# Softmax sums of an attention block taken off TensorE: transfers through DRAM and 32x32 transpositions in place of ones-matmuls

## The chip, the cores and the metric

The kernel runs on one core of a Trainium2 chip. The metric is the time of one execution on the device in microseconds (us). The profile is one execution as the hardware profiler records it. Its engines are PE (TensorE matmuls), PEld (TensorE weight loads, which overlap PE), DVE (VectorE), ACT (ScalarE), POOL (GpSimd) and SP (SyncE, which starts most of the transfers).

## The reference

The input x is 8 images of 64 channels and 64x64 pixels, float32. Layer 0 is attention over the 4096 pixels of each image, with a second, "unary" softmax that doesn't depend on the query:

```python
q = q - q_mean                      # q, k, v = 1x1 convolutions of x
k = k - k_mean
sim = softmax(einsum('bcn,bcm->bnm', q, k) / 8, axis=2)
out = einsum('bnm,bcm->bcn', sim, v)
unary = softmax(einsum('bc,bcm->bm', q_mean, k))
out = out + einsum('bcm,bm->bc', v, unary)[:, :, None]
x = x + out
```

Layer 1 takes the sign of the result, convolves it with binary weights of sizes 1, 3 and 5 with batch norm, adds the three, multiplies by a gate that is computed from the mean over each whole image, and adds its own input.

## The kernel before

Two images form a pair: image 0 has its channels on partitions 0 to 63, image 1 on 64 to 127. There are 4 pairs. For each pair there are 8 query blocks (`qb`) of 512 queries, so 32 blocks, numbered `g`. Within a block a loop of 32 slots `j` runs over the keys, 128 at a time. In each slot:

- `scores` computes the logits of 128 keys with 512 queries of both images into a PSUM tile `ps` (two buffers), four 64x64 matmuls in float32 (line 466), and ACT turns them into `e` with an exp (line 477). The pool `ep` has four buffers of `e`.
- `weighted` multiplies the values `v` with the `e` of the slot before and accumulates in `acc` (line 485), one buffer of two PSUM banks.
- `summed` adds that `e` to `es` on DVE (lines 498 and 500). At the end of the block `es` holds, for each query, 128 partial sums over keys, one on each partition.

Scores of slot j are issued before `weighted` and `summed` of slot j-1, so PE does not wait for the exp of its own slot. All orders are written out by hand: `attend` makes for each block a plan `at` of extra work by slot (`put(slot, function, ...)`), and each engine takes its instructions in that order.

At slot 0 of block g stands the work on older blocks. `weighted_out` copies `acc` of block g-1 to SBUF on ACT (line 507). `both` calls `mix_rows`: the query projection of block g+1 and, from g=3 on, the convolutions of block g-3, some 100 short bf16 matmuls (line 680). Their results lie in `z` tiles: two that share the `ps` pool, `z3` that takes the two banks of `acc`, and `z_5d` and `z1` in the two-buffer pool `ps_m`. ACT starts the row tile `sb` from `z_5d` (line 695) and copies `z3` out to `es_z` (`hold_rows`, line 720). DVE adds the others (`add_rows`, line 713); the parts kept in `es_z` are added later (`add_held`), and `end_rows` adds `z1` (line 729).

Then follow the sums of block g-1. `sums` multiplies `es` with ones on TensorE (line 516): four matmuls with 32 output columns each, one for each half of the queries of each image, so that each sum stands on 32 partitions. `reciprocals` inverts 128x256 values from PSUM on DVE in two halves (line 529, slots 4 and 6). `spread` copies them with eight SBUF to SBUF transfers on SP to the tile `r`, in which all 64 channels of an image have the reciprocals of its 512 queries (slot 7). `check_block` takes two signs with accumulation on ACT (line 409), which decide at the end whether a safe path is needed. `added` and `finish` (slots 10 and 12, lines 559 to 564) make x + out in `x2`. `signs_wide` and `signs` make the convolution's input from it, and `row_sums` its differences of rows (slots 17 and 19).

In blocks qb=2 the next pair's x is loaded. In blocks qb=3 `mean_part` sums it on DVE (line 278, slots 14, 18, 22, 26), and the eight output tiles of the pair before are finished on DVE and stored (`store`, line 796, every third slot from 3 on). At qb=4 `mean_scores` uses the sums. In blocks qb=4 to 7 `values` makes the next pair's value tiles, and `unary_part` adds the weighted values into `vu`. At qb=0 of that pair, `unary_end` sums `vu` over partitions, with four 128x1 matmuls, one for each 128 columns (line 355).

Of the kernel before, what the change touches and what calls it, by code (L numbers as in the profile page):

```python
# [18 lines left out]
F32 = mybir.dt.float32  # L19
# [3 lines left out]
ALU = mybir.AluOpType  # L23
AX = mybir.AxisListType
PSUM = bass.MemoryType.PSUM

P = 128
C = 64
# [3 lines left out]
QB = 512  # L32
NQ = N // QB
# [11 lines left out]
def conv_seq_kernel(ctx, tc, x, wq, wk, wv, vecs, w1, w3, w5, wtap, gw, out):  # L45
    nc = tc.nc
    n_pairs = x.shape[0] * x.shape[1] // P
    xf = x.rearrange("b c h w -> (b c) (h w)")
    of = out.rearrange("b c h w -> (b c) (h w)")
    img = [slice(0, C), slice(C, P)]  # L50
# [4 lines left out]
    ep = ctx.enter_context(tc.tile_pool(name="ep", bufs=4))  # L55
    fp = ctx.enter_context(tc.tile_pool(name="fp", bufs=1))
    sm = ctx.enter_context(tc.tile_pool(name="small", bufs=2))
    ps_s = ctx.enter_context(tc.tile_pool(name="ps_s", bufs=2, space=PSUM))
    ps_a = ctx.enter_context(tc.tile_pool(name="ps_a", bufs=1, space=PSUM))
    ps_m = ctx.enter_context(tc.tile_pool(name="ps_m", bufs=2, space=PSUM))  # L60

    def m_tile(name):
        return ps_m.tile([P, QB], F32, tag="m", name=name)
# [44 lines left out]
    make_identity(nc, ident)  # L108
    wu = cp.tile([P, P], F32, tag="wu", name="wu")
    nc.gpsimd.memset(wu, 0.0)  # L110

    fit = cp.tile([P, 2, n_pairs * (NQ + 1)], F32, tag="fit", name="fit")
    lim = cp.tile([P, 3], F32, tag="lim", name="lim")
# [140 lines left out]
    class Pair:  # L254
# [88 lines left out]
                nc.vector.tensor_tensor(self.vu, old, t, ALU.add)  # L343

        def unary_sum(self):
            su = self.tile(sm, "su2", 0, (P, 2))
            nc.vector.tensor_reduce(su, self.eu, AX.X, ALU.add)
            self.eub = self.tile(sm, "cl", "s")[:, 0:P]
            for b in range(2):
                nc.vector.tensor_scalar(self.eub[:, img[b]], ones[:, 0:C], su[:, b : b + 1], None, ALU.mult)  # L350

        def unary_end(self):
            po = self.po = m_tile(f"po_{self.name}")
            for t in range(4):
                nc.tensor.matmul(  # L355
                    po[:, 0:1], self.vu[:, bass.ts(t, P)], ones[:, 0:1], start=(t == 0), stop=(t == 3)
                )
            nc.tensor.matmul(po[:, 1:2], self.eub, ones[:, 0:1], start=True, stop=True)

        def unary_out(self):  # L360
# [145 lines left out]
            for c in parts:  # L506
                nc.scalar.copy(self.acc[qb][:, :, c], acc[:, :, c])  # L507

        def sums(self, qb):

            self.sums_p = m_tile(f"su_{self.name}_{qb}")
            es = self.es.pop(qb)
            for b in range(2):
                for h in range(2):
                    i = 2 * b + h
                    nc.tensor.matmul(  # L516
                        self.sums_p[32 * i : 32 * i + 32, 0 : QB // 2],
                        ones[:, 0:32],
                        es[:, b, bass.ts(h, QB // 2)],
                        start=True,  # L520
                        stop=True,
                        tile_position=(0, 32 * i),
                    )

        def reciprocals(self, qb, part):
            if part == 0:
                self.rc = self.tile(fp, "rc", qb, (P, QB // 2))
            c = bass.ts(part, P)
            nc.vector.reciprocal(self.rc[:, c], self.sums_p[:, c])  # L529

        def spread(self, qb):
            self.r[qb] = self.tile(fp, "r", qb)
            for b in range(2):
                for s in range(2):
                    for h in range(2):
                        i, o = C * b + 32 * h, C * b + 32 * s
                        nc.sync.dma_start(
                            out=self.r[qb][o : o + 32, bass.ts(h, QB // 2)], in_=self.rc[i : i + 32, :]
                        )


        def sums_wide(self, qb):
# [23 lines left out]
            )  # L566

        def check_block(self, qb, side):
            self.check(self.rc, int(self.name) * NQ + qb, (side,))


        def join(self):
# [358 lines left out]
    def attend(pairs):  # L931
# [9 lines left out]
        def plan(g):  # L941


            at = {}

            def put(i, f, *a):
                at.setdefault(i, []).append((f, a))

            pr, qb = divmod(g, NQ)

            def nx():
                return pairs[pr + 1]

            if g >= 1:
                p, b = block(g - 1)
                put(0, p.weighted_out, b)
            if qb == 3 and pr >= 1:
                put(0, pairs[pr - 1].gate)
            if qb == 4 and pr + 1 < n_pairs:
                put(0, lambda: nx().mean_scores())  # L960
                put(0, lambda: nx().mean_scores_out())
                put(1, lambda: nx().value_weights())
            if qb == 0 and pr >= 1 or g == 1:
                put(0, pairs[g // NQ].unary_end)
                put(0, pairs[g // NQ].unary_out)
            if g == 2:
                put(0, mean_rows_out)
            def both():
                q = block(g + 1) if g + 1 < n_blocks else None
                if g == 0:  # L970
                    mix(q, None)
                else:
                    mix_rows(q, rows(g - 3) if g >= 3 else None)

            put(0, both)
            if g >= 3:
                p3, b3 = block(g - 3)
                put(2, p3.add_held, b3, "AB")
                put(3, p3.add_held, b3, "SD")
                put(4, p3.end_rows, b3)  # L980
            if g >= 1:
                put(0, p.sums, b)
                for part in range(2):
                    put(4 + 2 * part, p.reciprocals, b, part)
                put(7, p.spread, b)
                put(8, p.check_block, b, 0)
                put(10, p.check_block, b, 1)
                put(10, p.added, b)
                put(12, p.finish, b)
                put(15, p.signs_wide, b, 2)  # L990
                put(17, p.signs_wide, b, 1)
                put(19, p.signs, b)
            if g + 2 < n_blocks:
                put(2, lambda: block(g + 2)[0].copy_x(block(g + 2)[1], (g + 2) // NQ * P))
            if 2 <= g < n_blocks - 1:
                p2, b2 = block(g - 2)
                put(17, p2.row_sums, b2)
                put(19, p2.row_sums3, b2)
            if g == n_blocks - 4:
                put(14, p.copy_tile)  # L1000
            if qb == 2 and pr >= 1:
                put(20, pairs[pr - 1].gate_mean)
            if qb == 3 and pr >= 1:
                for i in range(NQ):
                    put(3 + 3 * i, pairs[pr - 1].store, i, rows_of(pr - 1))
            if g == 0:
                for i in range(NQ):
                    put(max(4 * i - 1, 0), pairs[0].values, i)
                    put(4 * i + 1, pairs[0].unary_part, i)
                put(31, pairs[0].unary_sum)  # L1010
                for i, n in enumerate((2, 1, 0)):
                    put(8 + 8 * i, weight_mean, n)
                    put(12 + 8 * i, weight_scale, n)
            if g == 1:
                put(10, norms)
                put(11, mean_rows)
            if g == 2:
                for n in range(3):
                    put(12 + 5 * n, centre, n)
                    put(14 + 5 * n, weight_signs, n)  # L1020
                for i in range(2):
                    put(26 + 2 * i, weight_combinations, KS[1 + i])
            if pr + 1 < n_pairs:
                if qb == 2:
                    def begin():
                        pairs[pr + 1] = Pair(str(pr + 1), load_x(str(pr + 1), rows_of(pr + 1)))

                    put(1, begin)
                if qb == 3:
                    for c in range(4):  # L1030
                        put(14 + 4 * c, lambda c=c: nx().mean_part(c, quarters[c]))
                if qb >= 4:
                    for h in range(2):
                        i = 2 * (qb - 4) + h
                        put(14 + 8 * h, lambda i=i: nx().values(i))
                        put(17 + 8 * h, lambda i=i: nx().unary_part(i))
                    if qb == NQ - 1:
                        put(28, lambda: nx().unary_sum())
            if g == n_blocks - 1:
                put(1, pairs[-1].join)  # L1040
                put(22, lambda: mix(None, rows(n_blocks - 3), one_bank, score_banks))
                put(27, lambda: mix(None, (pairs[-1], pairs[-1].joint_rows(0, 6, 0)), one_bank, score_banks))
            return at
# [79 lines left out]

    nb_ = sm.tile([P, 1], F32, tag="nb", name="nb")
    nc.vector.tensor_reduce(nb_, fit, AX.XY, ALU.add)
    nc.vector.tensor_scalar(nb_, nb_, n_pairs * (NQ * QB + 2.0) + QB, None, ALU.is_equal)
    pb = m_tile("pb")
    nc.tensor.matmul(pb[:, 0:1], ones, nb_, start=True, stop=True)
    good = sm.tile([P, 1], I32, tag="good", name="good")
# [121 lines left out]
```

## Time and profile before

| | before |
|---|---|
| median of 3 runs | 1973.69 us (1970.32 to 1974.4) |
| run with the profile | 1970.24 us, span 1968.1 us |
| granted TensorE clock | 0.997 |
| SP transfers `r<-rc` (spread) | 248 of 32 KB, 1.9 us to landing |
| SP transfers `xc<-in_x` | 60 of 64 KB, 2.4 us to landing |
| SP transfers `out<-sb` | 28 of 256 KB, 2.1 us to landing |

In a line of a group the columns are: line of the kernel, engine, operation, written tile <- read tiles, shapes (partitions x elements), number of instructions, then busy time in us with the mean duration of one in ns, then the idle time of the engine just before them with what ended it. A wait is put down to what came last by the profile.

### The profile page before, as it was taken

The page shows a single profiled execution, that of the slowest core. Times are in us where ns is not written, and L with a number is a line of the kernel's source. Part 1 is how long each engine was busy: PE and PEld are TensorE (multiplying, and loading weights), DVE is VectorE, ACT ScalarE, POOL GpSimd, SP SyncE. Part 2 cuts the span into 40 slices and gives each one's busy share as a digit, 9 for nine tenths or more (in the row PEclk, how much of TensorE's full clock was granted, in tenths as well). Part 3 has the DMA queues.
Part 4 walks back from the last instruction along what each step waited for, and adds up shares of the span by engine and source line. Part 5 has one row for each costly group of instructions (what it writes and reads, how often), then busy time and mean ns, then how long its engine had stood idle before and what let it go on. Part 6 is the DMA issues. An engine that isn't in the chain of part 4 may idle for free.

```text
span 1968.1 us, 48733 instructions
## 1 busy us (share of the span) xinstructions
PE 1945.9 (99%) x21120; PEld 766.8 (39%) x21120; DVE 1627.1 (83%) x1976; ACT 1262.8 (64%) x1474; POOL 5.9 (0%) x26
## 2 busy tenths in 40 slices
PE   9999999999999999999999999999999999999997
PEld 4333343343333333343433333343343333333334
DVE  7878988888887798888788878888888888878876
ACT  5667666666666666666666665666666666666663
POOL 0000000000000000000000000000000000000000
PEclk9999999999999999999999999999999999999998
DMA  3010000000001010000002001000000000100001
GB/s 99 10 48 18 16 19 10 18 13 16 18 15 56 18 55 16 18 10 16 16 15 61 14 29 40 16 18 14 14 13 18 16 18 31 40 17 20 20 12 45
DMA packets 43373, 47.96 MB, mean 24 GB/s; under 512 B 16000, under 2 KB 32912, under 8 KB 43024
## 3 DMA queue, kind: packets, MB, share of 16 engines
q1 hardware_dynamic: 42400, 43.59, 8.4%
q8 instruction: 167, 2.74, 0.6%
q10 hardware_dynamic: 720, 1.18, 0.2%
q14 instruction: 54, 0.44, 0.1%
q0 software_dynamic: 32, 0.01, 0.0%
HBM read 14.89 MB, written 8.39 MB: 12 GB/s over the span
## 4 chain that ended last, share of the span: by engine, by line
PE 92%; DVE 5%; issue 1%; ACT 1%; DMA 0%; DVEq 0%; SPq 0%; ACTq 0%
PE ps L466 42%; PE acc L485 42%; PE z L680 4%; DVE es L500 4%; PE su L516 1%; PE pq L451 1%; PE pv L308 1%; PE z L751 1%; ACT e L477 1%; PE z_5d L680 0%; DMA x<-in_x 0%; DVE sb L796 0%; DVE sb L713 0%; PE warm L152 0%; PE po L355 0%
## 5 line engine op out<-in xcount | busy, mean ns | idle before, releaser
L477 ACT ACTIVATE e<-ps 128x1024 f32<-128x1024 f32 x1024 | 1049.8, 1025 | 619.1 <-PE ps L466 590.9
L500 DVE TENSOR_TENSOR es<-es,e 128x1024 f32<-128x1024 f32 x960 | 1171.2, 1220 | 184.4 <-ACT e L477 146.8
L466 PE MATMUL ps<-q,x 64*64 64x512 f32 x8192 | 1067.7, 591 | 0.9 <-DVE kb L162 0.9
L485 PE MATMUL acc<-e,v 64*64 64x512 f32 x8192 | 1064.2, 589 | 0.7 <-ACT e L477 0.3
L485 PEld LDWEIGHTS acc<-e,v 64*64 64x64 f32 x8192 | 309.5, 131 | 572.1 <-ACT e L477 307.0
L466 PEld LDWEIGHTS ps<-q,x 64*64 64x64 f32 x8192 | 307.8, 133 | 543.7 <-issue 287.9
L713 DVE SCALAR_TENSOR_TENSOR sb<-z,frac,sb 128x256 f32<-128x256 f32 x87 | 39.2, 478 | 62.6 <-PE z L680 62.6
L680 PE MATMUL z<-e,wt 64*64 64x256 bf16 x754 | 85.3, 272 | 0.1
L680 PE MATMUL z<-ec,wt 64*64 64x256 bf16 x754 | 85.3, 272 | 0.0
L680 PEld LDWEIGHTS <-wt 64*64 64x64 bf16 x1508 | 77.3, 106 | 1.1 <-issue 0.3
L680 PEld LDWEIGHTS <-wc 64*64 64x64 bf16 x1218 | 67.7, 107 | 3.6 <-issue 0.6
L498 DVE TENSOR_TENSOR es<-e,e 128x1024 f32<-128x1024 f32 x32 | 39.2, 1225 | 33.3 <-ACT e L477 33.3
L713 DVE SCALAR_TENSOR_TENSOR sb<-es_z,frac,sb 128x256 f32<-128x256 f32 x145 | 62.2, 480 | 0.0
L680 PE MATMUL z<-ec,wc 64*64 64x256 bf16 x464 | 62.0, 274 | 0.0
L529 DVE RECIPROCAL rc<-su 128x128 f32<-128x128 f32 x62 | 59.1, 953 | 0.0
L695 ACT ACTIVATE sb<-z_5d,shift,frac 128x256 f32<-128x256 f32 x58 | 29.6, 561 | 45.9 <-PE z_5d L680 45.9
L596 ACT ACTIVATE s<-x,vec 128x512 bf16<-128x512 f32 (+2 forms) x66 | 46.1, 702 | 5.2 <-DVE x L564 5.2
L680 PE MATMUL z<-e,wc 64*64 64x256 bf16 x319 | 45.4, 273 | 0.0
L458 DVE TENSOR_SCALAR q<-pq,mx 128x256 f32<-128x256 f32 x60 | 27.0, 480 | 16.7 <-PE pq L451 16.2
L507 ACT COPY o<-acc 128x1024 f32<-128x1024 f32 (+2 forms) x33 | 32.3, 981 | 1.2 <-PE acc L485 1.2
L409 ACT ACTIVATE ck<-rc,lim 128x256 bf16<-128x256 f32 x62 | 30.9, 498 | 0.0
L720 ACT COPY es_z<-z 128x1024 f32<-128x1024 f32 x29 | 29.3, 1012 | 0.0
(150 smaller groups left out, 698.3 us busy)
## 6 DMA issues: line engine op xcount, KB each, us to landing
r<-rc SPq DMA_DIRECT2D x248, 32.0 KB, 1.9
x<-in_x SPq DMA_DIRECT2D x15, 512.0 KB, 5.8
out<-sb SPq DMA_DIRECT2D x28, 256.0 KB, 2.1
ec<-e SPq DMA_DIRECT2D x29, 153.0 KB, 2.4
xc<-in_x SPq DMA_DIRECT2D x60, 64.0 KB, 2.4
ec<-e SPq DMA_DIRECT2D x29, 132.0 KB, 2.3
y<-y SPq DMA_DIRECT2D x30, 64.0 KB, 1.9
w_tap<-in_wtap SPq DMA_DIRECT2D x2, 560.0 KB, 9.8
```

The source lines that it names most:

```text
L409: nc.scalar.activation(junk[:, 0:w], r, AF.Sign, bias=lim[:, side : side + 1], scale=1.0 - 2.0 * side, accum_out=fit[:, side, i : i + 1],)
L466: nc.tensor.matmul(ps[img[h], b, :], self.x[img[b], bass.ds(j * P + h * H, H)], self.q[qb][img[b], :], start=True, stop=neg is None,)
L477: nc.scalar.activation(e, ps, AF.Exp, scale=1.0 / 8.0)
L485: nc.tensor.matmul(self.acc[qb][img[b], h, :], self.v[img[h], j, img[b]], e[img[h], b, :], start=(j == 0), stop=(j == NK - 1),)
L498: nc.vector.tensor_tensor(self.es[qb], self.first, e, ALU.add)
L500: nc.vector.tensor_tensor(self.es[qb], self.es[qb], e, ALU.add)
L507: nc.scalar.copy(self.acc[qb][:, :, c], acc[:, :, c])
L529: nc.vector.reciprocal(self.rc[:, c], self.sums_p[:, c])
L596: nc.scalar.activation(sy[n][0][:, rows, pad : pad + HH], self.x2[qb][:, r0 * HH : r1 * HH].rearrange("p (h w) -> p h w", w=HH), AF.Sign, ...
L680: nc.tensor.matmul(z[img[b], :].rearrange("p (h w) -> p h w", w=HH), taps[img[h], c * C : c * C + C], src[:, first : first + 3 * step + 1 ...
L695: nc.scalar.activation(sv[:, :, t, :], z.rearrange("p (j w) -> p j w", w=HH), AF.Identity, bias=shift, scale=frac[5][:, t : t + 1],)
L713: nc.vector.scalar_tensor_tensor(out, z.rearrange("p (j w) -> p j w", w=HH), by, out, ALU.mult, ALU.add)
```

## The change

The sums over keys leave TensorE. `es` has 128 partitions of partial sums for 1024 queries (2 images x 512). `send` writes it to DRAM, and `gather` reads it back in four transfers of 128 KB, so that each of the four groups of 32 partitions holds one quarter of the queries (256), with four values per query in each partition. `fold` adds the four on DVE, transposes squares of 32x32, adds the 32 elements of each row, which leaves 8 sums on each partition, takes the reciprocal of these, and transposes them back spread over 32 columns. `spread` writes one row of each group to DRAM and reads it back onto all 64 partitions of an image, with three transfers in place of eight.

The tile that receives the gathered sums comes from the pool of the `e` tiles. The check works on 8 values per partition. `add_held` and `end_rows` move to later slots, the `mean_part` calls move from qb=3 to qb=2 for pairs other than the first, and `vu` is folded to 128 columns on DVE, so that one matmul takes the place of four.

```diff
         def unary_sum(self):
+            for w in (2 * P, P):
+                nc.vector.tensor_tensor(
+                    self.vu[:, 0:w], self.vu[:, 0:w], self.vu[:, w : 2 * w], ALU.add
+                )
...
-            for t in range(4):
-                nc.tensor.matmul(
-                    po[:, 0:1], self.vu[:, bass.ts(t, P)], ones[:, 0:1], start=(t == 0), stop=(t == 3)
-                )
+            nc.tensor.matmul(po[:, 0:1], self.vu[:, 0:P], ones[:, 0:1], start=True, stop=True)
...
-        def sums(self, qb):
...
-        def reciprocals(self, qb, part):
...
+        def send(self, qb):
+            self.sent = self.tile(dp, "es", qb, (4, 32, 4, QB // 2))
+            nc.sync.dma_start(
+                out=self.sent.rearrange("g i q c -> (g i) (q c)"),
+                in_=self.es.pop(qb).rearrange("p b c -> p (b c)"),
+            )
+
+        def gather(self, qb):
+            self.parts = self.tile(ep, "e", f"parts_{qb}", (P, 4, QB // 2))
+            for q in range(4):
+                nc.sync.dma_start(
+                    out=self.parts[32 * q : 32 * q + 32, :, :],
+                    in_=self.sent[:, :, q, :].rearrange("g i c -> i g c"),
+                )
+
+        def fold(self, qb):
+            f, t = self.tile(fp, "fold", qb, (P, QB // 2)), self.parts[:, 0, :]
+            nc.vector.tensor_reduce(f, self.parts.rearrange("p g c -> p c g"), AX.X, ALU.add)
+            nc.vector.transpose(out=t, in_=f)
+            nc.vector.tensor_reduce(
+                rec, t.rearrange("p (k i) -> p k i", i=32), AX.X, ALU.add
+            )
+            nc.vector.reciprocal(rec, rec)
+
+            self.rc = self.tile(fp, "rc", qb, (P, QB // 2))
+            nc.vector.transpose(out=self.rc, in_=rec.unsqueeze(2).broadcast_to([P, 8, 32]))
 
         def spread(self, qb):
+            rows = self.tile(dp, "rc", qb, (4, QB // 2))
+            nc.sync.dma_start(out=rows, in_=self.rc[0:P:32, :])
             self.r[qb] = self.tile(fp, "r", qb)
             for b in range(2):
-                for s in range(2):
-                    for h in range(2):
...
+                nc.sync.dma_start(
+                    out=self.r[qb][img[b], :],
+                    in_=rows[2 * b : 2 * b + 2, :].rearrange("s c -> (s c)").unsqueeze(0).broadcast_to([C, QB]),
+                )
...
         def check_block(self, qb, side):
-            self.check(self.rc, int(self.name) * NQ + qb, (side,))
+            self.check(rec, int(self.name) * NQ + qb, (side,))
...
                 put(0, p.weighted_out, b)
+                put(0, p.send, b)
+                put(0, p.gather, b)
...
-                put(2, p3.add_held, b3, "AB")
-                put(3, p3.add_held, b3, "SD")
-                put(4, p3.end_rows, b3)
+                put(4, p3.add_held, b3, "AB")
+                put(6, p3.add_held, b3, "SD")
+                put(8, p3.end_rows, b3)
             if g >= 1:
-                put(0, p.sums, b)
-                for part in range(2):
-                    put(4 + 2 * part, p.reciprocals, b, part)
-                put(7, p.spread, b)
+                put(3, p.fold, b)
+                put(5, p.spread, b)
                 put(8, p.check_block, b, 0)
...
-                if qb == 3:
+                if qb == (3 if pr == 0 else 2):
                     for c in range(4):
                         put(14 + 4 * c, lambda c=c: nx().mean_part(c, quarters[c]))
```

More of the change, by code (lines that the diff above doesn't have):

```diff
@@ L57, in conv_seq_kernel @@
     sm = ctx.enter_context(tc.tile_pool(name="small", bufs=2))
+    dp = ctx.enter_context(tc.tile_pool(name="dram", bufs=2, space=bass.MemoryType.DRAM))
     ps_s = ctx.enter_context(tc.tile_pool(name="ps_s", bufs=2, space=PSUM))
@@ L110, in conv_seq_kernel @@
     nc.gpsimd.memset(wu, 0.0)
+    rec = cp.tile([P, 8], F32, tag="rec", name="rec")
     fit = cp.tile([P, 2, n_pairs * (NQ + 1)], F32, tag="fit", name="fit")
@@ L507, in weighted_out @@
                 nc.scalar.copy(self.acc[qb][:, :, c], acc[:, :, c])
-        def sums(self, qb):
-            self.sums_p = m_tile(f"su_{self.name}_{qb}")
-            es = self.es.pop(qb)
-            for b in range(2):
-                for h in range(2):
[L515 to L523, printed above, removed]
@@ L525, in reciprocals @@
-        def reciprocals(self, qb, part):
[L526 to L529, printed above, removed]
+        def send(self, qb):
[4 more added lines that the diff above has]
+            )
@@ L531, in spread @@
         def spread(self, qb):
+            rows = self.tile(dp, "rc", qb, (4, QB // 2))
+            nc.sync.dma_start(out=rows, in_=self.rc[0:P:32, :])
             self.r[qb] = self.tile(fp, "r", qb)
             for b in range(2):
-                for s in range(2):
[L535 to L539, printed above, removed]
+                nc.sync.dma_start(
+                    out=self.r[qb][img[b], :],
+                    in_=rows[2 * b : 2 * b + 2, :].rearrange("s c -> (s c)").unsqueeze(0).broadcast_to([C, QB]),
+                )
@@ L1125, in conv_seq_kernel @@
     nc.vector.tensor_reduce(nb_, fit, AX.XY, ALU.add)
-    nc.vector.tensor_scalar(nb_, nb_, n_pairs * (NQ * QB + 2.0) + QB, None, ALU.is_equal)
+    nc.vector.tensor_scalar(nb_, nb_, n_pairs * (16.0 * NQ + 2.0) - 16.0 + 2 * QB, None, ALU.is_equal)
     pb = m_tile("pb")
```

## The prediction

> **What bounds the kernel now.** I read the page's busy shares first, then the chain that ended last, then the groups of instructions, and last the timeline of one start of a block, since the change acts there.
>
> ```profile
> PE 1945.9 (99%) x21120; PEld 766.8 (39%) x21120; DVE 1627.1 (83%) x1976; ACT 1262.8 (64%) x1474; POOL 5.9 (0%) x26
> ...
> PE 92%; DVE 5%; issue 1%; ACT 1%; DMA 0%; DVEq 0%; SPq 0%; ACTq 0%
> ```
>
> TensorE holds 92% of the chain, so matmul time that is removed can count in full, and VectorE at 83% has room on average. The 5% on DVE is not spread evenly: in the list of the chain's pieces it lies in two stretches, 677 to 732 us and 1161 to 1216 us. These are the blocks qb=3 of pairs 1 and 2. From the starts of the conv products I read 58.96 us for a plain block, 60.0 with value tiles, 61.9 with the unary term, but 63.2 and 63.6 for those two. The groups that the change touches:
>
> ```profile
> L516 PE MATMUL su<-es,ones 128*32 128x256 f32 x248 | 19.8, 391 | 0.5
> L529 DVE RECIPROCAL rc<-su 128x128 f32<-128x128 f32 x62 | 59.1, 953 | 0.0
> L355 PE MATMUL po<-ones,vu 128*128 128x1 f32 x32 | 4.2, 253 | 0.0
> L278 DVE TENSOR_REDUCE xs<-x 128x1 f32<-128x1024 f32 x14 | 17.0, 1214 | 2.0 <-DMA x<-in_x 2.0
> ```
>
> And a block's start, from the timeline (start, duration, engine, line, operation, tiles, count, idle before):
>
> ```profile
> 792.83 1.23 DVE L500 TENSOR_TENSOR es<-es,e 128x1024 f32<-128x1024 f32 x1 [0.49 <-ACT e L477]
> ...
> 796.43 1.02 ACT L695 ACTIVATE sb<-z_5d,shift,frac 128x256 f32<-128x256 f32 x2 [1.02 <-PE z_5d L680]
> ...
> 797.23 0.27 PE L680 MATMUL z<-e,wt 64*64 64x256 bf16 x1
> 797.40 1.01 ACT L720 COPY es_z<-z 128x1024 f32<-128x1024 f32 x1
> ...
> 797.51 0.64 PE L516 MATMUL su<-es,ones 128*32 128x256 f32 x8
> 797.61 0.88 DVE L713 SCALAR_TENSOR_TENSOR sb<-z,frac,sb 128x256 f32<-128x256 f32 x2 [1.96 <-PE z L680]
> ...
> 798.08 1.09 PE L466 MATMUL ps<-q,x 64*64 64x512 f32 x8
> ...
> 798.99 1.04 PE L485 MATMUL acc<-e,v 64*64 64x512 f32 x8
> ```
>
> The reader is to see: the sums stand between the last conv product and the next scores on PE; the next `weighted` (798.99) writes the `acc` banks, which hold the conv's z3 until ACT's copy L720 ends at 797.40 + 1.01 = 798.41.
>
> [...] The trace, whose transfers start on SP, has 1.9 us for 32 KB, 2.1 for a 256 KB store and 4.3 for the first of four queued 512 KB loads[...]. [...] The built order has that wait: the gather on SP waits for the landing of send. So the two latencies add. [...] No transpose is in this trace.
>
> **The change, part by part.**
>
> *Sums off TensorE.* Without them the first scores follow the last products: groups of products start 0.11 us apart, so 797.23 + 0.11, with some fill 797.4, instead of 798.08: 0.7 us. But `weighted` would then be due at 797.4 + 0.91 = 798.3, and the banks come free at 798.41, plus 0.06 for the signal (e ends 791.07, weights start 791.13) and about 0.1 for weights: 798.58. Before it began at 798.99. I take 0.40 us a block, not 0.7: the sums stood half in the shade of the z3 copy. The following scores (about 799.44) need the banks whose last reader is L713, ended 799.26: no wait. 26 blocks (29 with convs less the three with stores) by 0.40 = 10.4 us. The first two blocks have no conv: 2 x 0.6 = 1.2 us.
>
> *Fold on VectorE.* Reduction of 1024 elements 1.22, [...] reciprocal of 8 some 0.18 (a 128x1 one takes 0.17)[...]; each waits for the one before, 0.06 as between the dependent adds: 2.9 us. It replaces two reciprocals spaced 0.87: 1.74. So +1.15 us a block. Bounds: 2.3 if all but the reduction run at 0.3; 4.6 if the strided reduction and the transpositions take twice per element. [...] An ordinary block has DVE near 50 us busy in 59 to 60, and by its middle DVE has caught up again (824.84 waits for ACT), so this is hidden behind PE. Queued behind the fold are the adds of e tiles, for which the exps wait through the four e buffers: an exp four tiles later needs the add. An exp starts every 1.72 us, and exp plus add take 2.3, so the slack is 4 x 1.72 - 2.3 = 4.6 us plus PE's own slack of about 0.4. By adding up the DVE rows from 799.3 on, the lag at slot 12 is about 3 us: held.
>
> *Transfers.* es is complete at 792.83 + 1.23 = 794.06. Send moves 512 KB: [...] by the 256 KB store 2.1 + 0.8 = 2.9; upper end 4.3. Then four gather issues at about 0.63 (as the eight r issues, 5.0 us) put the fourth 1.9 us after; it lands in about 2.4 (as xc), upper end 3.5 in 1 KB pieces. Sum 0.1 + 3.0 + 1.9 + 2.4 = 7.4 us: 801.5; upper end 9.9: 803.9. The fold stands in DVE's order behind the add of e tile 2, which ends near 802.7, so it finds its data. What waits: `parts` is an e buffer, and in the built order it passes to e tile 5, whose exp waits for the fold's second reduction. Fold 802.7 + 2.2 = 804.9; that exp is due about 805.7 (806.16 before, less 0.4). 0.8 us to spare, 1.2 with PE's slack; so the fold may begin as late as 803.9. Spread is two more latencies, 2 + 3 us from 805.6, and r is used seven slots later, near 819: hidden. The check on 8 columns saves ACT 0.6 us, off the path.
>
> *Mean sums from qb=3 to qb=2.* In the stretch from 677.08 to 733.3 DVE worked without a pause, 56.2 us. Out go four reductions spaced 1.13 (702.10 to 703.23): 4.5; in comes 1.15: 52.9, starting near 676.6, so to 729.5. PE's own pace would have the last add end at 671.51 + 58.96 - 0.61 - 0.40 = 729.46. So these blocks become about even, 59.4 on average of 63.4: 2 x 4.0 = 8.0 us. The third store block, pair 3, has no mean sums and took 58.96; I charge it 0.3. Block qb=2 gets 4.5 and has no stores (eight spaced 0.67, 5.3): 52.1, below 52.9, hidden.
>
> *Unary term.* Three of four 128x1 matmuls go: 1459.25 to 1460.14 for four, so 0.66 a pair, 2.6 us over four. Two small adds are hidden at slot 28 of DVE.
>
> Sum: 10.4 + 1.2 + 8.0 - 0.3 + 2.6 = 21.9 us. 1973.69 - 21.9 = 1952 us.
>
> **The rivals.** A: the transfers come late. Fifth exp, and with it PE, wait in all 31 blocks. If the gather lands at 805.5, 1.6 us after the limit, 31 x 1.6 = 50 us: 1952 + 50 = 2002, slower than before. For it: two chained latencies on 512 KB, pieces of 1 KB, DVE blocked meanwhile. Against: my upper end is 803.9. B: the fold is at its dear end, 4.6 us. Ordinary blocks lose about 0.5 by the release of the buffer (26 x 0.5 = 13), store and mean blocks 1 us more each (5): 1970. C: the z3 copy doesn't bind and PE gains 0.9 a block, the 0.64 of the sums and the 0.29 that the view gives as the wait of their weights for ACT L695: 26 x 0.5 = 13 more: 1939. Against it: L720 can start no earlier than L695 ends.
>
> **How the numbers follow.** Forecast 0.62, A 0.14, B 0.14, C 0.10. The range goes from 1938, with C, to 1971, with B; it leaves out A and the tails, some 0.18. Faster by over 0.2% means below 1969.7: the forecast, C and over half of B, 0.82. Same 0.05, from B and a slight A. Slower 0.13, from A.
>
> **What would show it.** Right: no L516 group; PE still above 98%; `weighted` after z3 waiting for ACT L720 with a real gap; the fold's reduction without idle time for a DMA; blocks at 58.6 and 59.6; the qb=3 blocks near 59.4. Wrong: idle DVE before the fold released by a DMA, an ACT wait for DVE at e tile 5 in every block, or plain blocks at 58.96 or more; or a fold of over 4 us.

## The result and the profile after

The changed kernel takes 1956.14 us (median of 4 runs, 1955.96 to 1956.36) against 1974.05 us of the kernel before (1970.32 to 1975.08), measured beside it. The ratio is 0.9913, 95% interval 0.9896 to 0.993: 17.9 us faster, where 21.9 were forecast. The spans of the two profiles differ by less, 1968.1 to 1953.9 = 14.2 us. The profile of before is that of its shortest run (1970.24 us), and its runs spread over 5 us, those of the changed kernel over 0.4. The sums below, block by block, are of these two traces, so they must come to 14.2.

From the page of the changed kernel, engines, chain and two groups:

```profile
PE 1927.4 (99%) x20848; PEld 810.3 (41%) x20848; DVE 1683.2 (86%) x2077; ACT 1249.1 (64%) x1474; POOL 5.9 (0%) x26
...
PE 87%; DVE 6%; ACT 5%; issue 1%; DMA 1%; SPq 0%; DVEq 0%; ACTq 0%
...
L533 DVE TENSOR_REDUCE fold<-e_parts 128x256 f32<-128x1024 f32 x31 | 60.7, 1958 | 3.6 <-DMA e_parts<-es 3.6
L732 ACT COPY es_z<-z 128x1024 f32<-128x1024 f32 x29 | 29.3, 1011 | 0.0
```

PE is still busy all the time, but it holds 87% of the chain and no longer 92%: ACT came in with 5%, of which the start of `sb` and the copy of z3 make 2.9. The fold's first reduction takes 1.96 us, far from the 1.22 assumed; waiting for transfers costs VectorE only 3.6 us before 3 of 31 folds (g=1, 2 and 4). Where time is waited for, from the view of waits of the changed kernel (who <- for whom: total us, times, longest):

```profile
PEld acc L489 <- ACT es_z L732: 28.3, 29, 1.0
ACT e L481 <- DVE es L504: 16.9, 20, 1.3
ACT e L481 <- DVE rec L535: 8.1, 6, 2.6
PEld pm L288 <- DVE xm L286: 5.3, 3, 2.3
DVE fold L533 <- DMA e_parts<-es: 3.6, 3, 1.8
```

Every one of the 29 blocks with convolutions waits with the weights of its first `weighted` for the z3 copy. The exps wait for DVE in a few blocks, and the fold's end (L535) in six. Now the start of a plain block (timeline of the changed kernel, columns as before):

```profile
793.86 1.01 ACT L732 COPY es_z<-z 128x1024 f32<-128x1024 f32 x1
...
794.92 0.21 PEld L489 LDWEIGHTS acc<-e,v 64*64 64x64 f32 x8 [1.00 <-ACT es_z L732]
794.92 1.09 PE L489 MATMUL acc<-e,v 64*64 64x512 f32 x8
795.24 0.48 DVE L725 SCALAR_TENSOR_TENSOR sb<-z,frac,sb 128x256 f32<-128x256 f32 x1
795.84 0.24 PEld L470 LDWEIGHTS ps<-q,x 64*64 64x64 f32 x8 [0.71 <-issue]
795.87 1.09 PE L470 MATMUL ps<-q,x 64*64 64x512 f32 x8
...
799.21 1.96 DVE L533 TENSOR_REDUCE fold<-e_parts 128x256 f32<-128x1024 f32 x1
801.21 0.45 DVE L534 STREAM_TRANSPOSE e_parts<-fold 128x256 f32<-128x256 f32 x1
801.68 0.42 DVE L535 TENSOR_REDUCE rec<-e_parts 128x8 f32<-128x256 f32 x1
...
802.38 0.45 DVE L541 STREAM_TRANSPOSE rc<-rec 128x256 f32<-128x256 f32 x1
802.75 1.18 DVE L504 TENSOR_TENSOR es<-es,e 128x1024 f32<-128x1024 f32 x1
```

Two things stand here. `weighted` begins when the z3 copy has ended (793.86 + 1.01 = 794.87). And the second scores load their weights at 795.84, just after the last addition that reads the score banks, L725, has ended at 795.72: a second gate, though the view puts that idle time to "issue". The fold takes from 799.21 to 802.75, 3.54 us. It finds its data: VectorE doesn't wait before it.

The time of a block is measured here from one start of the ACT copy of `acc` (L507, after L511) to the next:

| blocks | before, us | after, us | sum of differences, us |
|---|---|---|---|
| 20 others, pair 0 from qb=3 on (plain 58.96, with values 60.00) | | 58.58, 59.60 | -7.8 |
| three at qb=0 with the unary term | 60.89 | 59.83 | -3.2 |
| the first two, g=1 and 2 | 58.13, 57.76 | 58.35, 57.42 | -0.1 |
| pair 0, qb=4 (g=4) | 60.83 | 62.83 | +2.0 |
| pair 1, qb=3 and 4 | 61.23, 63.54 | 61.24, 61.11 | -2.4 |
| pair 2, qb=3 and 4 | 61.22, 65.05 | 61.25, 61.11 | -3.9 |
| pair 3, qb=3 | 60.51 | 61.26 | +0.7 |
| before the first and after the last | | | +0.5 |

Together -14.2. The plain blocks came as forecast, and so did the unary term in the three blocks at qb=0; the fourth, pair 0's, lies in g=1, where it is lost again. Most of what is missing lies in the blocks with stores and those after them, in g=4 of pair 0 and in the first two.

### The profile page after: what moved, and what is told of

It is laid out like the page before. It is cut to its first block, busy times and chain, and to the rows that moved or that the text cites. A ratio compares the mean times of both kernels' runs of the same rounds, so it can differ in the third digit from the quotient of the medians.

```text
span 1953.9 us, 48347 instructions
## 1 busy us (share of the span) xinstructions
PE 1927.4 (99%) x20848; PEld 810.3 (41%) x20848; DVE 1683.2 (86%) x2077; ACT 1249.1 (64%) x1474; POOL 5.9 (0%) x26
## 3 DMA queue, kind: packets, MB, share of 16 engines
q1 hardware_dynamic: 58024, 76.22, 12.8%
## 4 chain that ended last, share of the span: by engine, by line
PE 87%; DVE 6%; ACT 5%; issue 1%; DMA 1%; SPq 0%; DVEq 0%; ACTq 0%
PE acc L489 41%; PE ps L470 40%; DVE es L504 4%; PE z L692 2%; ACT sb L707 1%; ACT es_z L732 1%; ACT e L481 1%; PE pq L455 1%; PE pv L311 1%; PE z L763 1%; DMA e_parts<-es 1%; PE z_5d L692 0%; DVE fold L533 0%; DMA x<-in_x 0%; DVE sb L725 0%
## 5 line engine op out<-in xcount | busy, mean ns | idle before, releaser
L470 PE MATMUL ps<-q,x 64*64 64x512 f32 x8192 | 1094.8, 591 | 0.9 <-DVE kb L165 0.9
L489 PE MATMUL acc<-e,v 64*64 64x512 f32 x8192 | 1086.7, 590 | 7.6 <-ACT e L481 4.6
L489 PEld LDWEIGHTS acc<-e,v 64*64 64x64 f32 x8192 | 325.7, 131 | 570.5 <-ACT e L481 297.6
L470 PEld LDWEIGHTS ps<-q,x 64*64 64x64 f32 x8192 | 348.7, 133 | 501.0 <-issue 271.4
L725 DVE SCALAR_TENSOR_TENSOR sb<-z,frac,sb 128x256 f32<-128x256 f32 x87 | 39.2, 478 | 61.8 <-PE z L692 61.8
L533 DVE TENSOR_REDUCE fold<-e_parts 128x256 f32<-128x1024 f32 x31 | 60.7, 1958 | 3.6 <-DMA e_parts<-es 3.6
L725 DVE SCALAR_TENSOR_TENSOR sb<-es_z,frac,sb 128x256 f32<-128x256 f32 x145 | 62.2, 479 | 0.0
L511 ACT COPY o<-acc 128x1024 f32<-128x1024 f32 (+2 forms) x33 | 32.3, 981 | 1.2 <-PE acc L489 1.2
L311 PEld LDWEIGHTS pv<-wx,x 64*64 64x64 f32 x1024 | 22.3, 134 | 17.1 <-issue 8.8
```

The costliest lines, as they stand in the source:

```text
L311: nc.tensor.matmul(pv[img[h], b, i * w : (i + 1) * w], self.x[img[b], bass.ds((4 * g + i) * P + h * H, H)], self.wx[img[b], :], start=True ...
L470: nc.tensor.matmul(ps[img[h], b, :], self.x[img[b], bass.ds(j * P + h * H, H)], self.q[qb][img[b], :], start=True, stop=neg is None,)
L489: nc.tensor.matmul(self.acc[qb][img[b], h, :], self.v[img[h], j, img[b]], e[img[h], b, :], start=(j == 0), stop=(j == NK - 1),)
L533: nc.vector.tensor_reduce(f, self.parts.rearrange("p g c -> p c g"), AX.X, ALU.add)
L725: nc.vector.scalar_tensor_tensor(out, z.rearrange("p (j w) -> p j w", w=HH), by, out, ALU.mult, ALU.add)
```

## The experiments

The theory at this point: (1) what is missing is DVE time, since the fold is 3.54 us, not 2.9; (2) in plain blocks TensorE is held at the block's start by what reads the PSUM banks, not by its own work. The rivals: the transfers are late; the mean sums' move did nothing, or everything.

**The fold's first reduction by contiguous additions** (e1)

```diff
-            nc.vector.tensor_reduce(f, self.parts.rearrange("p g c -> p c g"), AX.X, ALU.add)
+            half = self.parts[:, 0:2, :]
+            nc.vector.tensor_tensor(half, half, self.parts[:, 2:4, :], ALU.add)
+            nc.vector.tensor_tensor(f, t, self.parts[:, 1, :], ALU.add)
```

> The changed kernel, with the fold's first reduction (over a stride of 1 KB, 1.96 us a piece in its trace) made by two additions of contiguous columns, 512 and 256 wide. Theory 1 (what is lost against the forecast is VectorE time of the fold in the blocks with stores, and in the one of pair 0 with mean sums): the fold becomes about 0.8 us shorter, plain blocks stay at 58.58 us, and the blocks with stores and those after them lose 0.5 to 1 us each, so 2 to 5 us in all: 1951 to 1954. Theory 2 (these blocks wait for the transfers of the sums, not for VectorE): no change beyond 0.5 us.

1950.28 us, ratio to before 0.9878 (0.9862 to 0.9895); 5.9 us less than the changed kernel. The tile view of the gathered sums in this run (durations in ns: least, median, most):

```profile
L534 DVE TENSOR_TENSOR e_parts<-e_parts x31: 683/684/693, 83.3 to 1864.4; 128x512 f32<-128x512 f32 x31
L535 DVE TENSOR_TENSOR fold<-e_parts x31: 424/424/426, 84.0 to 1865.1; 128x256 f32<-128x256 f32 x31
```

0.68 + 0.42 in place of 1.96. Most plain blocks keep 58.58. g=4 falls from 62.83 to 60.99, the qb=3 blocks from 61.25 to 60.44 (pairs 1 and 2) and 60.79 (pair 3), g=1 and 2 from 58.35 and 57.42 to 57.23 and 56.88. So it was VectorE's time. In the blocks with stores no fold waits for its data in either trace, so the theory of late transfers falls there; in g=1, 2 and 4 the fold still waits for them, 1.45, 0.47 and 1.21 us in this run.

**The mean sums, undone and alone** (e2, e3)

e2 is the changed kernel, e3 the kernel before, each with this one line:

```diff
# e2
-                if qb == (3 if pr == 0 else 2):
+                if qb == 3:
# e3
-                if qb == 3:
+                if qb == (3 if pr == 0 else 2):
```

> The changed kernel, with the mean sums back in the qb=3 blocks for every pair. Theory 1 (VectorE bounds the blocks with stores, and the move makes room for the fold there): each of the two pairs pays the 4.5 us of reductions again, with the 1.8 us more of the fold on top of what before showed; 9 to 12 us slower than the changed kernel: 1965 to 1968. Rival (the move is worth little, the gain comes from TensorE alone): less than 3 us, 1959 at most.

> The kernel before, with nothing but the mean sums moved to the qb=2 blocks of pairs 1 and 2. Theory 1: the qb=3 blocks and those after them fall to about 60.5 and 60.8 us, which takes away 3.4 us for pair 1 and 4.9 for pair 2: 8 us faster than before, so almost half of what the whole change brought. Rival (the gain is from TensorE alone): under 2 us.

e2: 1964.72 us, 8.6 more than the changed kernel, a little under the 9 to 12 expected, and still 0.9952 of before (0.9936 to 0.9969). e3: 1962.96 us, 0.9943 of before (0.9926 to 0.9959), 11.0 us by the medians. In its trace the four blocks qb=3 and 4 of pairs 1 and 2 take 60.51, 60.82, 60.51 and 60.82, 8.4 us less than in the trace of before, and all others are unchanged within 0.1. So the move alone is worth about as much as all the rest of the change (e2, 9.2 us by the medians). By the medians the two would add up to 20.2, where the change has 17.9; by the traces they add up to 7.3 + 6.1 = 13.4, where it has 14.2. The runs spread too widely to say whether the two hinder each other.

**What holds a block's start** (e4, e7, e8)

```diff
# e4 and e7
-            nc.scalar.copy(self.z3, two)
+            nc.scalar.copy(self.z3[:, 0, :], two[:, 0, :])
...
-                put(6, p3.add_held, b3, "SD")
# e7 and e8
-            for n in "SAB":
+            for n in "AB":
                 p.add_rows(qb, 5, n, z[5, n])
```

> The changed kernel, which copies only half of z3 (A and B) out of PSUM and leaves out the additions of the other half (S and D of the 3x3 convolution), so its output lacks those terms. It asks whether the z3 copy on ScalarE holds back the first weighted matmul of a block. Theory 1 (it does): the copy ends 0.46 us earlier, the gap before that matmul goes, plain blocks fall from 58.58 to about 58.3, 27 x 0.27 = 7 us; the 1.6 us less of VectorE helps the blocks with stores by 2 to 4 more: 1945 to 1948. Rival (the copy is not what holds it; TensorE is at its own pace): plain blocks stay at 58.5 or more, and only the blocks with stores gain, 1952 to 1955.

> As the run with half of the z3 copy, and without the two additions of S of the 5x5 convolution besides, so the output lacks these terms too. In that run plain blocks stayed at 58.58 us with a wait of the second scores for VectorE's additions. Theory (two gates one behind the other: the z3 copy, and behind it the four additions that read the score banks): with both open, plain blocks fall by 0.2 to 0.3 us, to 58.3. Rival (TensorE is at its own pace there): 58.58 again.

> The changed kernel without the two additions of S of the 5x5 convolution (its output lacks that term); the z3 copy is whole. It opens the second gate alone. Theory (two gates): the first weighted matmul still waits for the copy, the second scores no longer for VectorE: plain blocks 58.45 to 58.5, the 0.12 us of the first gate staying. Rival (only the z3 copy counts): 58.58.

All three leave terms out of the result: S and D of the 3x3 convolution, S of the 5x5, or both. Plain blocks: 58.58 us in the changed kernel, 58.58 with the half copy, 58.49 without the additions of S, 58.15 with both edits. In e4 the copy was 0.59 us long and `weighted` began earlier, but the next step took it all back. The timeline of e4:

```profile
789.57 0.58 ACT L732 COPY es_z<-z 128x512 f32<-128x512 f32 x1
...
790.22 1.16 PE L489 MATMUL acc<-e,v 64*64 64x512 f32 x8
...
791.58 1.09 PE L470 MATMUL ps<-q,x 64*64 64x512 f32 x8 [0.20 <-DVE sb L725]
```

The wait is now named: the second scores wait for VectorE's additions. My expectation for e4 was wrong by this, and its 1949.51 us come from the blocks that DVE bounds. Each gate alone yields 0.00 or 0.09 us, both 0.43: two readers of PSUM that end at nearly the same point of the block. That VectorE has less to do is not the reason, since e1, which also takes work from it, keeps 58.58. e7 (1940.68 us) and e8 (1952.08) ran once each.

**How close the transfers are** (e5)

```diff
-                put(3, p.fold, b)
+                put(2, p.fold, b)
```

> The changed kernel with the fold one slot earlier (2 in place of 3), to see when the gathered sums land in a plain block: there VectorE comes to the fold first and waits for them. In the first block, where it waits already, they landed 7.8 us after the end of the sums (76.22 to 84.00). Theory 1 (the same 7.8 us in every block, about 0.9 us before the fold needs them at slot 3): an idle of 1.1 us before the fold in nearly every block; the receiving buffer now goes to e tile 4, whose exp then starts about 0.75 us late, of which TensorE feels 0.35: 10 us more, 1966. Rival (the transfers are done long before): no idle before the fold, and no loss: 1954 to 1958.

1967.73 us in a single run, close to the 1966 of theory 1. From the tile view of the gathered sums in this run:

```profile
  DMA e_parts<-es: 34.7, 24
who waited for it (us, times):
  ACT e L481: 38.8, 23
```

24 of 31 folds wait for their data, and 23 exps then wait for the fold. From the end of the last addition into `es` to the start of a fold that waited, the timeline of this run gives a median of 7.8 us, 22 of the 24 between 7.1 and 8.6, and two of 9.2 and 10.8. In the changed kernel a plain block reaches the fold 8.7 us after that end (790.51 to 799.21), so the transfers have about 0.9 us to spare; one slot earlier they are the bound.

**A faster version** (e9, e10)

e9 is e1 with two more edits: the last reduction of the mean sums right after its parts, and the stores later.

```diff
+                    put(27, lambda: nx().mean_sum())
...
-                    put(3 + 3 * i, pairs[pr - 1].store, i, rows_of(pr - 1))
+                    put(9 + 3 * i, pairs[pr - 1].store, i, rows_of(pr - 1))
```

> The kernel with the fold by contiguous additions, in which the last reduction of the next pair's mean sums is done right after them (slot 27), so that TensorE's matmul with them doesn't wait behind the queue of VectorE at qb=4, and in which the stores start at slot 9 in place of 3, when the fold's backlog is past. Theory 1: the waits of 0.6, 0.6 and 0.3 us before that matmul go, and half of what is lost in the middle of the store blocks: 1947 to 1949. If a later store pushes the backlog to the end of the block and it costs there what it saves: 1950, as without it.

1947.87 us, 0.9876 of before (0.9859 to 0.9892). g=4 falls to 60.45, qb=3 and 4 of pairs 1 and 2 to 60.13 and 60.45, pair 3's to 60.13. TensorE no longer idles for `xm`. Pair 3's block has no mean sums, so its step from 60.79 to 60.13 is the work of the later stores alone.

e10 opens both gates with the whole result computed:

```diff
+            nc.vector.tensor_copy(self.z5, two.rearrange("p b c -> p (b c)")[:, QB // 2 :])
...
-            for n in "SAB":
-                p.add_rows(qb, 5, n, z[5, n])
+            p.hold_five(qb, t5)
...
-            seqs[1] += products(5, "A") + products(5, "D") + products(5, "B")
+            seqs[1] += a5[0:6] + products(5, "D") + a5[6:] + products(5, "B")
```

> The fastest kernel so far (contiguous fold, early last reduction, later stores), with both gates at a block's start opened and the whole result computed: the products of D of the 5x5 convolution come earlier and the 1x1 product last, so that ScalarE ends the z3 copy about 0.3 us earlier, and VectorE frees the score banks with one copy of 768 columns (0.96 us estimated from 1.22 for 1024) in place of four additions (1.66 us), which it makes later from SBUF. Theory (two gates): plain blocks at 58.15 to 58.3 us, 29 blocks by 0.3 to 0.4: 1935 to 1939; VectorE has 0.9 us more a block, which may cost the three store blocks up to 1 us each. Rival (the earlier D products wait for the bank of the query projection and TensorE loses there what it gains): 1945 or more.

1940.33 us (1940.2 to 1940.38), 0.9831 of before (0.9814 to 0.9849): the fastest, 33 us under before. The copy of 768 columns takes 0.96 us. The timeline of a block's start:

```profile
844.92 1.01 ACT L739 COPY es_z<-z 128x1024 f32<-128x1024 f32 x1
...
845.99 0.21 PEld L494 LDWEIGHTS acc<-e,v 64*64 64x64 f32 x8 [0.70 <-ACT es_z L739]
...
846.47 0.15 PEld L475 LDWEIGHTS ps<-q,x 64*64 64x64 f32 x4 [0.28 <-DVE e_z L743]
846.90 1.04 PE L475 MATMUL ps<-q,x 64*64 64x512 f32 x8
```

The second scores follow `weighted` by 0.91 us (845.99 to 846.90), where they took 0.95 in the changed kernel: the second gate is all but open. The weights for `weighted` still wait for the z3 copy, 0.70 against 1.00. Plain blocks take 58.31, not the 58.15 of e7, hence 1940 where 1935 to 1939 was expected: the earlier D products bring the copy only part of the way.

## Why the prediction came out as it did

The 17.9 us of the medians stand nearer to the forecast of 21.9 than its working deserves. The working was done on a trace, and on the traces the gain is 14.2, so the sum was 7.7 too high: 2.5 in the mean sums, 2.4 in g=4, 1.7 in the first two blocks (0.6 of it the unary term of pair 0), and 1.2 in the third store block, the two ends and roundings. The medians come nearer because the other runs of before were longer than its profiled one, 1974.05 against 1970.24; the forecast knew nothing of that, so this part is luck.

- **Sums off TensorE, 0.40 us a block.** Right in size: 58.96 to 58.58, and 60.00 to 59.60. That the z3 copy ends the gain early was right, but only half the reason: "no wait" for the second scores was wrong. They start right after L725, and e4 shows that this alone keeps the same 58.58. Rival C, without the z3 gate, would not have come true for this reason.
- **First two blocks, 2 x 0.6.** Failed: they gained 0.1 together. They have no convolutions, so slot 3 comes sooner, and here rival A held: the fold waited 1.76 and 0.78 us, and one exp in each block 2.6 and 1.5 us for the fold. In e1 the fold is 0.86 us shorter. In g=2 it still waits 0.47 us, but no exp waits for it any more, and the block gains 0.9 us; in g=1 it waits 1.45, and the gain of 0.9 is mostly the unary term. So late data and a long fold cost the gain together. The timeline of g=1 of the changed kernel:

```profile
75.00 1.22 DVE L504 TENSOR_TENSOR es<-es,e 128x1024 f32<-128x1024 f32 x1
...
84.00 1.96 DVE L533 TENSOR_REDUCE fold<-e_parts 128x256 f32<-128x1024 f32 x1 [1.76 <-DMA e_parts<-es]
```

- **Transfers, 7.4 us.** 7.8 in this block (76.22 to 84.00), median 7.8 in e5. The mechanism and the size hold in plain blocks, whose folds have no wait. The 3.0 for the send was the author's estimate; the gather was issued 2.7 to 3.5 us after the send in 30 of 31 blocks of the changed kernel. Four gather issues took 1.74 us in the blocks shown, less than the 2.5 assumed; the steps after them were not measured apart.
- **Fold, 2.9 us.** Mis-sized: 3.54. The transpositions took 0.45 each, the reduction of 256 took 0.42. An estimate from the additions in the trace of before, 0.686 us for 512 columns (L559) and 1.220 for 1024 (L500), gives 0.42 for 256 columns; that a transposition would go at that rate too was the author's estimate, which no trace of before shows. The term that failed is the reduction over four columns 1 KB apart. The forecast took for it the 1.22 of a contiguous reduction of 1024 (L278, 1.214), as if the stride made no difference, which was an estimate too; the trace has 1.96. The whole fold stays inside the range that was kept to 4.6.
- **Mean sums moved, 8.0 us, and 0.3 lost in the third store block.** The right mechanism, too large a size. Before to after, pairs 1 and 2 gained 6.3 in two blocks each, of which 0.8 belongs to the two plain gains counted elsewhere: 5.5. Pair 3 lost 0.7. In the forecast's own measure (starts of the conv products) the qb=3 blocks of pairs 1 and 2 fell from 63.2 and 63.6 to 61.3, not to 59.4; e3, the same move without the fold, has 59.9. The early backlog of 3.54 us at slot 3 collides with the first stores, as e9 shows; the prediction only asked whether DVE's total fits in the block. In the changed kernel's qb=3 block exps wait in the middle, and at the end `xm` stands behind the queue:

```profile
690.53 1.02 ACT L481 ACTIVATE e<-ps 128x1024 f32<-128x1024 f32 x1 [1.26 <-DVE es L504]
...
719.58 10.52 DVE L504 TENSOR_TENSOR es<-es,e 128x1024 f32<-128x1024 f32 x8
730.02 0.15 DVE L286 TENSOR_REDUCE xm<-xs 128x1 f32<-128x4 f32 x1
```

- **A term that was missing.** Pair 0 keeps its mean sums in qb=3, beside the fold. The sum counted its next block, g=4, as plain; it became 2.0 us longer. Two waits meet there that before did not have. TensorE stands idle for `xm` for 1.46 us, and the fold waits 1.07 us for its data, since the gather starts 5.05 us after the send, in all other blocks 2.7 to 3.5. So rival A came true in this block too:

```profile
251.14 0.34 SPq L518 DMA_DIRECT2D es<-es  x1
256.19 1.74 SPq L526 DMA_DIRECT2D e_parts<-es  x4
261.78 1.97 DVE L533 TENSOR_REDUCE fold<-e_parts 128x256 f32<-128x1024 f32 x1 [1.07 <-DMA e_parts<-es]
```

  e1 (60.99) shortens the first wait to 0.29 us; in e9 (60.45) neither is left. Why this one send is slow is not shown.
- **Unary term, 0.66 us a pair.** 60.89 to 59.83 is 1.06, of which 0.39 is the plain gain: 0.67. The forecast counted it four times; in g=1, the fourth, the wait for the fold takes it back.

One cost was in no one's sum. In the trace of before TensorE stands idle for `xm` at qb=4 of pairs 1 and 2 for the same 2.6 us, yet the two blocks take 63.54 and 65.05. The longer one ran just after the wait at a granted clock of 0.50, the other at 1.00. From the view by stretches, 1.06 us behind the end of the wait of pair 2 and 0.62 behind that of pair 1 (the last three numbers are the granted clock, the DMA share and GB/s):

```profile
1218.00:1219.00 1.00, 1.00 (x22) 0.90 (x18) 0.64 (x2) 0.00 (x0) 0.00 (x0) 0.50 0.00 0
734.00:735.00 1.00, 1.00 (x32) 0.87 (x30) 0.61 (x3) 0.00 (x0) 0.00 (x0) 1.00 0.00 0
```

In the trace of e2, which has the same two waits, it is pair 1's block that is longer, 64.79 against 63.16, and again its clock is 0.50. In the other traces no wait for `xm` is over 1.5 us, and the clock falls only at the program's end. So what the move of the mean sums brings has two parts, a shorter wait and, in some blocks, a clock that does not fall.

What stays open: what decides whether the clock falls, and how much of the 5 us of spread in before it makes. The runs of before fit it, 1970.2 and 1970.7 us at a mean clock of 0.997 and six of 1974.0 to 1976.3 at 0.994, but only the first of these has a trace. It isn't the only source: e4 and e9, which don't have the long waits, still spread over 3.2 and 1.8 us.

## What to carry to other kernels

Here 0.64 us of matmul time went from a block's start, and the block became 0.38 us shorter, since two readers of PSUM still had to end, the z3 copy and the addition L725: ask for each of the next matmuls which copy or addition frees its bank. When work moves to an engine with room on average (VectorE was 83% busy), lay its backlog over the work that is queued in the same slots; a total that fits in the block says little about the middle, as in the qb=3 blocks of pairs 1 and 2, which took 61.3 us where 59.4 was forecast. A transfer chain is hidden by the time up to its first user: 8.7 us in a plain block for a chain of 7.8, but in g=1, which has no convolutions, VectorE came 1.76 us too early.

## What the runs showed of the hardware

A VectorE reduction of 128x1024 float32 to one column over contiguous data took 1.21 us (the mean sums); one to 256 columns over four values 1 KB apart took 1.96. Whether the stride or the short rows cost it was not separated. Two contiguous additions did the same in 0.68 + 0.42. A 512 KB store to DRAM and its gathering back in four transfers of 1 KB pieces took 7.1 to 8.6 us in most blocks of e5, and 10.8 in the longest. After two of the four waits of 2.6 us that TensorE had in before and e2, the granted clock was 0.50, in before for about 3.4 us (estimated from stretches of 1 us), and the block 1.5 or 1.6 us longer.
